# Gated outputs of batches 1 and 3 of each group: ScalarE scale and GpSimd add in the place of one VectorE instruction

## The chip, the cores and the metric

The kernel runs on one core of one Trainium2 chip. The time is the device time of that core in microseconds (us). The engines are named as in the profile: PE (TensorE; PEld is its weight load), DVE (VectorE), ACT (ScalarE), POOL (GpSimd), SP (SyncE, which issues most DMAs). [...]

## The reference

The input `x` has 16 batches of 128 tokens of 128 features, the context 16 x 77 x 128. Four layers follow each other, each with a gated cross attention and a gated feed-forward part:

```
for layer in 0..3:
    x = x + tanh(g_xattn[layer]) * attention_layer(layernorm(x), context)
    x = x + tanh(g_ffn[layer])   * ffn_layer(layernorm(x))
```

Attention has 16 heads in layers 0 to 2 and 8 in layer 3. Layer 0 multiplies its softmax by a given array `gp`. The feed-forward parts differ: in layer 0 eight experts with a threshold and a capacity, in layer 1 one expert and a second norm, in layer 2 an MLP rounded to 8 bits, in layer 3 eight experts of which each token takes one, so that tokens are sorted by expert.

## The kernel before

**Tiling.** The batches are cut into 4 groups `g` of 4 batches `i` (0 to 3). The running `x` stays in SBUF for the whole kernel: `x[g]` is a part of the tile `token[g]` (so profiles call it token), and `x[g][:, i, :]` is a tile of 128 tokens x 128 features in f32. Matrix outputs come into 4 PSUM banks of tag M, scores into 2 double banks of tag S.

**One attention group.** Layers 0 and 1 go through `small_group` (two half passes of 8 heads for each batch), layers 2 and 3 through `big_group` and `big_pass` (layer 2 has two passes of 8 heads, layer 3 has one). For each group `layer_norm` runs: statistics (DVE, L500), a few small steps (POOL, L507 to L529, and ACT, L517 and L519), the scaling to `xn` (L537 on ACT or L539 on DVE). Then `transposed` (PE tp L630, copied out at L470 on ACT or L472 on DVE). For each batch: scores S (PE, L844 or L995), their maximum and difference (DVE, L652 and L654), the exponential (ACT, L859 or L1004), sums (DVE, L864 or L1008), weighing (`gp` in layer 0 at L876, the reciprocal sums in layers 2 and 3 at L1015, on POOL or DVE), five transposes T (PE, L670) and copies to pT (ACT L470, L677 and L678, or DVE L472, L680 and L681), the product with the values. In layers 0 and 1 the reciprocal sums are spread on POOL or DVE (L887) and transposed (PE r_ps L891, copied at L895); the product O (L905) is multiplied by them on DVE (L910), and the output projection is y (L914). In layers 2 and 3 the projection is folded into the values, and y (L1021) is the product itself.

**The gate.** `gate` (L713) ends each batch and pass: one DVE instruction reads y from PSUM, multiplies it by tanh(g) and adds x, and writes x. There are 80 of these: 16 in layers 0, 1 and 3 each, 32 in layer 2. The layer norm of the next part of the layer reads all four batches of the group.

**Fillers.** Work on the context that does not depend on x, the folding of values for later layers (f_ps, L1506) and later keys (k_ps, L1678), is laid between. Layer 0's experts (h_ps L1810, y L1835) follow; some of their outputs already go the way ACT (L1848) and POOL (L1852 to L1854). At the end layer 3 sorts tokens: POOL scatters rows (L1361) to memory (rowsA for groups 0 and 1, rowsZ for 2 and 3), SP fetches blocks of rows, each goes through one expert (T L1947, h_ps L1956, y L1971), and POOL scatters the results to the output (L1980).

**What sets the order.** Every step is a node of `Work`, made by `add(at, engine, cost, fn, reads, writes, new)`, with a due time `at`, an engine or a choice of two, and a cost. `layout` is a list scheduler which runs before the program is built: it takes, of the nodes that can start, that with the earliest due time, and of two engines the one that is done first by its costs. The order that comes out is the order on each engine's queue. A node that reads a PSUM bank of tag M is due 6 units earlier. `NUDGES` shifts due times: each entry (first, count, hundredths) moves `count` nodes from `first` on; with count 0 it shifts the choice between two engines. The order on each engine is fixed when the kernel is built, and on the chip each engine takes its queue in order and waits where it must.

```
    FLEX = ("ACT", "DVE")
    ...
    add(t, WEIGH, WEIGH_COST, weigh, reads=[prk, rk], writes=[pwk], new=[("pwb", pwk)])
    ...
    add(t + 3, "DVE", 0.35, lambda i=i: gate(layer, g, i, own["y", i]), reads=[yk, ("x", g, i)], writes=[("x", g, i)])
```

Of the kernel before, what the change touches and what calls it, by code (L numbers as in the profile page):

```python
# [11 lines left out]
F32 = mybir.dt.float32  # L12
# [5 lines left out]
AF = mybir.ActivationFunctionType  # L18
ALU = mybir.AluOpType
# [3 lines left out]
P = 128  # L23
B = 16
D = 128
# [41 lines left out]
WVO = 3  # L67

# [8 lines left out]
    (1513, 6, -124), (798, 0, -181), (993, 1, -236), (1260, 1, -247), (2453, 0, -108), (1719, 2, -59), (1367, 0, -126), (993,  # L77
    6, -14), (291, 1, 107), (1571, 8, -54), (995, 1, -39), (309, 2, 221), (1529, 2, 213), (69, 4, 154), (976, 8, -55), (2180,
    4, 100), (2873, 6, -282), (995, 1, -46), (1861, 2, 51), (990, 4, -210), (741, 8, -112), (2360, 1, -288), (978, 6, -216),
    (999, 1, -97), (991, 1, -233), (1574, 1, 276), (2391, 1, 113), (987, 1, -302), (314, 8, 43), (2248, 8, -106), (861, 3,  # L80
    -155), (1142, 1, -166), (961, 1, -107), (983, 1, -234), (85, 1, 291), (1672, 4, 383), (1776, 4, -115), (2702, 8, -139),
    (1080, 3, -218), (987, 1, -109), (2728, 8, -80), (2064, 5, -279), (629, 4, 293), (336, 4, 212), (1709, 8, -65), (1048, 5,
    -247), (993, 1, 184), (742, 1, -98), (1454, 8, -130), (2724, 1, -276), (1521, 4, -278), (2207, 2, -197), (1469, 4, 62),
    (1763, 4, -247), (1520, 4, 118), (1233, 5, -233), (993, 4, 82), (1450, 6, 129), (1752, 0, -87), (2015, 0, -184), (1856,
    2, 150), (2468, 8, -390), (684, 0, -169), (2392, 6, 93), (934, 8, -326), (2721, 5, -263), (955, 1, -59), (2393, 1, -157),
    (1558, 0, -169), (1165, 0, -87), (2670, 8, -100), (2053, 0, -93), (2713, 4, -389), (961, 1, 44), (2051, 0, -126), (1993,
    4, -190), (739, 4, -167), (2308, 8, -75), (1981, 3, -237), (997, 1, -77), (948, 6, -63), (927, 8, -241), (957, 1, -52),
    (989, 3, -107), (977, 1, -150), (863, 1, 231), (2123, 1, 19), (2393, 1, 245), (2617, 4, -147), (658, 6, -53), (749, 1,
    -123), (67, 3, 289), (2690, 2, -380), (240, 4, 232), (945, 8, -73), (991, 1, 366), (997, 2, -83), (1440, 2, 180), (2021,
    1, 215), (989, 1, -132), (140, 2, 49), (2309, 4, -53), (995, 1, -35), (1676, 2, -133), (2474, 1, 237), (1001, 1, -68),  # L90
    (435, 8, 52), (2038, 4, -272), (585, 8, -283), (1675, 8, 120), (1718, 1, -396), (2152, 4, -272), (1046, 1, -307), (1754,
    2, -131), (1019, 5, -246), (852, 8, -297), (2005, 1, 104), (2393, 1, -89), (959, 1, -48), (1752, 8, 283), (2039, 5, -92),
    (974, 5, -9), (1015, 1, -67), (2393, 1, 125), (590, 0, -190), (973, 1, 13), (399, 5, -103), (2019, 1, -272), (949, 6,
    -152), (1683, 8, 40), (973, 1, -6), (1142, 1, 114), (1846, 4, 181), (1008, 4, 94), (337, 1, -32), (1005, 1, -170), (1172,
    0, -143), (955, 4, -41), (1783, 1, -182), (961, 1, -80), (2039, 6, -99), (1759, 5, -219), (581, 1, 164), (1759, 1, -268),
    (1001, 6, 24), (2484, 8, -256), (2475, 0, -193), (1757, 1, -245), (1662, 0, -75), (993, 2, 39), (2791, 6, -257), (1841,
    1, -161), (2393, 1, -66), (1581, 1, -220), (793, 0, -167), (1724, 1, -289), (1048, 1, -50), (584, 2, -262), (85, 6, -97),
    (2041, 2, 94), (2042, 4, 273), (1071, 8, -234), (578, 8, -39), (948, 5, 242), (412, 0, -161), (998, 2, 19), (1558, 8,
    -35), (2006, 0, -187), (2336, 4, -88), (2062, 1, 301), (1171, 8, 330), (1753, 4, -285), (1009, 3, -81), (2520, 4, 334),
    (1712, 5, -268), (757, 2, -48), (1014, 4, -105), (1166, 4, -383), (987, 2, 157), (1760, 8, 166), (1831, 4, 298), (1342,  # L100
    4, -369), (978, 4, 68), (989, 2, 220), (2565, 1, -363), (1001, 1, -116), (951, 3, -32), (341, 0, 185), (2065, 0, -177),
    (2269, 8, -327), (1015, 1, 34), (975, 2, -29), (747, 1, -57), (1740, 0, -107), (977, 1, -53), (966, 2, -25), (1013, 8,
    -54), (979, 1, -25), (386, 8, -205), (1003, 1, -88), (956, 2, -39), (453, 4, -276), (1514, 8, -112), (337, 1, -100),
    (953, 1, 57), (1642, 2, 385), (1003, 1, -37), (2155, 1, 187), (1046, 1, -256), (1778, 4, -39), (1982, 4, 236), (1565, 8,
    -75), (997, 2, -40), (1028, 1, 113), (993, 1, 48), (2485, 0, -178), (1460, 5, -246), (501, 2, 258), (1030, 1, -71), (742,
    1, 206), (2032, 0, -102), (977, 2, 22), (985, 1, -261), (2832, 6, -192), (337, 2, 103), (979, 4, -45), (2340, 1, -238),
    (1532, 8, -141), (742, 1, -79), (991, 1, 59), (747, 1, -134), (977, 1, 92), (998, 6, 34), (2722, 4, 319), (950, 4, -28),
    (2391, 1, 47), (948, 6, -33), (989, 1, -148), (997, 1, 101), (1684, 8, -120), (2557, 4, -242), (963, 1, -57), (336, 3,
    -107), (1028, 2, -148), (1005, 1, 209), (977, 1, -81), (959, 1, -39), (1740, 2, -302), (749, 1, -56), (749, 1, 56), (975,
    1, -77), (2186, 4, -238), (764, 1, -159), (1003, 1, -67), (977, 6, 105), (967, 1, -101), (956, 4, 31), (1013, 1, -67),  # L110
    (1046, 1, -161), (1535, 5, -90), (979, 1, -70), (1001, 1, 132), (1334, 4, -298), (1614, 3, -294), (959, 1, -45), (970, 2,
    -70), (993, 1, 58), (1005, 1, -126), (1255, 5, 161), (1008, 4, -78), (1545, 8, 310), (953, 2, 128), (984, 4, 47), (1527,
    1, -380), (958, 4, 98), (971, 2, -55), (2240, 1, -203), (997, 1, 31), (987, 1, 46), (373, 8, -112), (1003, 1, -15),
    (2216, 2, 131), (957, 1, -93), (2312, 2, -129), (714, 1, -234), (953, 4, 39), (2567, 1, -290), (1045, 5, 56), (997, 1,
    -56), (997, 2, 32), (369, 2, 100), (389, 0, -187), (1630, 1, 178), (2049, 6, -149), (744, 1, -102), (76, 8, -293), (1003,
    1, 58), (1929, 1, -214), (499, 5, -180), (456, 8, 328), (1009, 4, 74), (1005, 1, -61), (2042, 1, -226), (767, 1, -230),
    (2048, 5, -300), (2485, 8, 315), (961, 1, 29), (995, 2, -57), (2472, 6, 167), (2722, 1, -303), (2079, 8, -110), (1075, 2,
    131), (1269, 8, 150), (2045, 8, 298), (974, 4, 35), (2215, 6, -148), (1889, 2, 114), (1847, 8, 306), (1931, 1, -276),
    (682, 4, 336), (985, 1, -304), (1276, 4, 250), (970, 2, 69), (2567, 1, -242), (763, 4, -202), (989, 1, 65), (388, 5,
    -223), (995, 1, 66), (1011, 1, -250), (501, 4, -244), (1009, 3, -78), (1896, 1, 317), (1001, 4, -67), (857, 2, 172),  # L120
    (1275, 5, -157), (1013, 1, 104), (1997, 1, -179), (965, 1, -45), (1737, 4, 106), (1010, 4, -23), (2126, 2, -29), (1025,
    5, 138), (1047, 6, -61), (999, 1, -55), (2183, 2, 10), (1014, 2, 154), (1165, 4, 130), (1011, 8, -18), (2126, 3, 78),
    (638, 1, -189), (1015, 4, -128), (1010, 4, -80), (2186, 1, -234), (2580, 8, 281), (2869, 8, 365), (1587, 6, -123), (65,
    8, 60), (975, 4, 17), (1528, 5, -105), (979, 1, 179), (1009, 1, 34), (1984, 2, -283), (966, 5, 75), (995, 1, -52), (2519,
    2, 238), (2208, 1, -124), (1509, 8, -88), (2186, 1, -237), (1433, 8, -45), (2643, 4, 134), (1673, 1, -169), (1050, 4,
    137), (1019, 1, 168), (299, 2, -222), (437, 5, -50), (2415, 1, 252), (2348, 5, -96), (2277, 1, -267), (388, 4, 268),
    (2462, 2, -226), (962, 3, -300), (1005, 2, 97), (96, 0, -195), (695, 1, -300), (1446, 1, -218), (430, 1, -232), (642, 0,
    -156), (1379, 4, 379), (418, 8, 127), (2205, 2, -322), (967, 4, -103), (2336, 3, -227), (467, 5, -105), (374, 8, 127),
    (2108, 5, -69), (1003, 1, 92), (444, 3, 36), (989, 1, -81), (1046, 1, 158), (975, 1, -139), (389, 0, -199), (963, 8, 42),
    (1050, 1, -198), (2358, 1, -102), (1001, 1, -122), (965, 4, -43), (1929, 1, -152), (2128, 4, -301), (953, 4, -93), (975,  # L130
# [198 lines left out]
def kernel(ctx: ExitStack, tc: tile.TileContext, io):  # L329
# [382 lines left out]
    def gate(layer, g, i, y):  # L712
        nc.vector.scalar_tensor_tensor(x[g][:, i, :], y, tg[:, layer:layer + 1], x[g][:, i, :],  # L713
                                       op0=ALU.mult, op1=ALU.add)
# [1393 lines left out]
```

## Time and profile before

| what | value |
|---|---|
| median of 3 runs | 658.76 us (658.31 to 660.65) |
| the profiled execution's own time | 661.02 us |
| its span in the profile | 659.3 us |
| mean granted PE clock | 0.982 |
| busy: PE, DVE, ACT, POOL | 609.3, 525.2, 418.0, 326.2 us |
| DVE gates (L713) | 80, 26.4 us busy, 332 ns each |

The profile is of one execution, and its own time is above the median of the runs. A group's line gives the source line, the engine, the operation, tiles out<-in, their shapes and the count; then busy time and mean duration of one; then the time that the engine sat idle before these instructions, and what ended it. [...] "issue" is time in which an engine waited for nothing that the profile shows.

### The profile page before, as it was taken

The page shows a single profiled execution, that of the slowest core. Times are in us where ns is not written, and L with a number is a line of the kernel's source. Part 1 is how long each engine was busy: PE and PEld are TensorE (multiplying, and loading weights), DVE is VectorE, ACT ScalarE, POOL GpSimd, SP SyncE. Part 2 cuts the span into 40 slices and gives each one's busy share as a digit, 9 for nine tenths or more (in the row PEclk, how much of TensorE's full clock was granted, in tenths as well). Part 3 has the DMA queues.
Part 4 walks back from the last instruction along what each step waited for, and adds up shares of the span by engine and source line. Part 5 has one row for each costly group of instructions (what it writes and reads, how often), then busy time and mean ns, then how long its engine had stood idle before and what let it go on. Part 6 is the DMA issues. An engine that isn't in the chain of part 4 may idle for free.

```text
span 659.3 us, 16387 instructions
## 1 busy us (share of the span) xinstructions
PE 609.3 (92%) x5795; PEld 437.4 (66%) x5795; DVE 525.2 (80%) x1241; ACT 418.0 (63%) x1095; POOL 326.2 (49%) x773
## 2 busy tenths in 40 slices
PE   4888999999999999889899999999999998799895
PEld 3465666566444788555647678686667867599894
DVE  6888999994571459898998999998999999887442
ACT  3555668577666554767687857655585858347553
POOL 8687566541100106714453726528444646756653
PEclk9988999999999999998999999999999999879999
DMA  8894456748545553589574937669963532667573
GB/s 220 250 272 129 117 145 166 202 113 256 138 121 160 170 193 99 157 221 282 176 208 141 268 102 216 207 183 292 306 191 104 158 99 63 195 164 196 154 209 84
DMA packets 169179, 117.48 MB, mean 178 GB/s; under 512 B 12649, under 2 KB 159984, under 8 KB 169098
## 3 DMA queue, kind: packets, MB, share of 16 engines
q1 hardware_dynamic: 166650, 112.55, 60.1%
q0 software_dynamic: 1728, 3.17, 1.3%
q8 instruction: 46, 0.75, 0.5%
q10 hardware_dynamic: 720, 0.71, 0.4%
q14 instruction: 35, 0.29, 0.1%
HBM read 61.43 MB, written 55.89 MB: 178 GB/s over the span
## 4 chain that ended last, share of the span: by engine, by line
PE 29%; DVE 12%; POOL 7%; DMA 3%; issue 3%; ACT 2%; POOLq 0%; DVEq 0%; SPq 0%
PE y L1021 5%; PE T L670 4%; PE q_ps L951 4%; PE y L1082 2%; PE S L995 2%; POOL out_x L1980 2%; DVE pr L654 2%; DVE mx L652 2%; PE h_ps L1061 2%; PE h_ps L1956 2%; PE y L1971 1%; DVE sb L1008 1%; PE O L905 1%; DMA row<-rowsZ 1%; PE h_ps L1120 1%
## 5 line engine op out<-in xcount | busy, mean ns | idle before, releaser
L654 DVE TENSOR_TENSOR pr<-S,mx 128x616 f32<-128x616 f32 x112 | 89.6, 800 | 7.7 <-DVE mx L652 0.5
L652 DVE TENSOR_REDUCE mx<-S 128x8 f32<-128x616 f32 x112 | 87.6, 782 | 5.7 <-PE S L844 3.9
L1015 POOL TENSOR_TENSOR pw<-pr,rinv 128x616 f32<-128x616 f32 x41 | 50.0, 1225 | 71.1 <-DVE rinv L1010 33.9
L670 PE MATMUL T<-ident,pw 128*128 128x128 f32 (+1 forms) x400 | 64.0, 285 | 2.8 <-POOL pw L1015 2.5
L1021 PEld LDWEIGHTS y<-v,pT 128*128 128x128 f32 (+1 forms) x480 | 58.8, 194 | 7.4 <-issue 3.6
L1021 PE MATMUL y<-v,pT 128*128 128x128 f32 (+1 forms) x480 | 63.0, 281 | 0.2 <-DVE pT L681 0.2
L670 PEld LDWEIGHTS T<-ident,pw 128*128 128x128 f32 (+1 forms) x400 | 46.9, 143 | 23.3 <-issue 11.9
L470 ACT COPY pT<-T 128x384 f32<-128x384 f32 x99 | 46.6, 481 | 23.0 <-PE T L670 22.5
L859 ACT ACTIVATE pr<-pr 128x616 f32<-128x616 f32 x64 | 46.1, 723 | 16.0 <-DVE pr L654 15.6
L1840 DVE SCALAR_TENSOR_TENSOR token<-y,sc,token 128x128 f32<-128x128 f32 x96 | 32.9, 350 | 26.6 <-PE y L1835 23.9
L876 POOL TENSOR_TENSOR pw<-pr,gp 128x616 f32<-128x616 f32 x28 | 39.2, 1401 | 25.5 <-ACT pr L859 15.2
L864 DVE TENSOR_REDUCE ss<-pr 128x8 f32<-128x616 f32 x64 | 49.1, 783 | 1.4 <-ACT pr L859 1.4
L951 PE MATMUL q_ps<-xT,wq 128*128 128x512 f32 x96 | 48.1, 605 | 0.7 <-ACT xT L470 0.7
L677 ACT COPY pT<-T 128x128 f32<-128x128 f32 x97 | 26.7, 275 | 26.8 <-PE T L670 26.4
L470 ACT COPY vs<-f_ps 122x512 f32<-122x512 f32 (+3 forms) x56 | 32.8, 585 | 16.9 <-PE f_ps L1506 16.2
L1980 POOL DMA_INDIRECT out_x<-bo,row x30 | 29.8, 992 | 24.7 <-DVE bo L1975 19.8
L1004 ACT ACTIVATE pr<-pr 128x616 f32<-128x616 f32 x48 | 34.2, 717 | 8.0 <-DVE pr L654 7.6
L537 ACT ACTIVATE xn<-token,ln_b,ln_r 128x128 f32<-128x128 f32 x86 | 35.3, 487 | 6.2 <-POOL ln_b L529 4.0
L1506 PE MATMUL f_ps<-vz,ctxT 128*122 128x512 f32 (+3 forms) x80 | 39.1, 600 | 0.0
L1008 DVE TENSOR_REDUCE sb<-pr 128x8 f32<-128x616 f32 x48 | 37.5, 782 | 1.1 <-ACT pr L1004 1.1
L995 PE MATMUL S<-k,q 64*64 64x77 f32 x1536 | 36.0, 235 | 0.4 <-DVE pr L654 0.4
L995 PEld LDWEIGHTS S<-k,q 64*64 64x64 f32 x1536 | 31.1, 136 | 7.6 <-issue 3.2
(355 smaller groups left out, 1502.7 us busy)
## 6 DMA issues: line engine op xcount, KB each, us to landing
v<-folded SPq DMA_DIRECT2D x48, 320.0 KB
vx<-apart SPq DMA_DIRECT2D x32, 320.0 KB
apart<-vz SPq DMA_DIRECT2D x32, 308.0 KB
rowsA<-blank SPq DMA_DIRECT2D x15, 516.0 KB
rowsZ<-blank SPq DMA_DIRECT2D x15, 516.0 KB
kept<-ks SPq DMA_DIRECT2D x24, 308.0 KB
k<-kept SPq DMA_DIRECT2D x12, 616.0 KB
folded<-vs SPq DMA_DIRECT2D x21, 308.0 KB
```

Source lines behind the costliest of these rows:

```text
L470: nc.scalar.copy(out, src)
L652: nc.vector.tensor_reduce(mx, S4, axis=AX.X, op=ALU.max)
L654: nc.vector.tensor_tensor(pr.rearrange("p (a c) k -> p a c k", a=2), S4, mx.unsqueeze(3).to_broadcast([P, 2, 4, SK]), ALU.subtract)
L670: nc.tensor.transpose(own[jkey][:n, c, :], flat[:, lo:lo + n], ident)
L859: nc.scalar.activation(own["pr", i, half], own["pr", i, half], AF.Exp)
L864: nc.vector.tensor_reduce(own["s", i][:, 8 * half:8 * half + 8], own["pr", i, half], axis=AX.X, op=ALU.add)
L951: nc.tensor.matmul(own["q_ps", c], lhsT=wq()[:, (c0 + c) * P:(c0 + c + 1) * P], rhs=mem["xT"], start=True, stop=True)
L995: nc.tensor.matmul(S[rows64, a, c * SK:(c + 1) * SK], lhsT=own["q"][at, c, i * P + 64 * b:i * P + 64 * b + 64], rhs=own["k"][at, c, i * SK ...
L1008: nc.vector.tensor_reduce(s, own["pr", i], axis=AX.X, op=ALU.add)
L1015: eng.tensor_tensor(own["pw", i], own["pr", i], own["rinv", i].unsqueeze(2).to_broadcast([P, 8, SK]), ALU.mult)
L1021: nc.tensor.matmul(own["y", i], lhsT=own[u + (i, "pT", c // 3)][:n, c % 3, :], rhs=own["v", i][:n, c, :], start=(c == 0), stop=(c == 4))
L1980: ins = nc.gpsimd.indirect_dma_start(out=io["out"].rearrange("b s d -> (b s) d"), out_offset=bass.IndirectOffsetOnAxis(ap=own["row"][:, 2 ...
```

## The change

A table says which batches of a layer go the new way: batches 1 and 3 of every group in all layers. For these `gate` makes two nodes. ACT copies y out of PSUM and scales it by tanh(g) into a new SBUF tile `gt` (3 buffers), and POOL adds this tile to x. The other batches keep the DVE instruction. Both callers of `gate` now pass the due time and a function for y. The scale node reads a PSUM bank, and so is due 6 units earlier, as the DVE node is; the add on POOL does not.

`NUDGES` is another list: 733 entries for 597. Node numbers move since each changed gate is two nodes; a part of the old entries is kept under new numbers, others are dropped, many are new.

```diff
+BY_TWO = ((1, 3), (1, 3), (1, 3), (1, 3))
...
-    def gate(layer, g, i, y):
-        nc.vector.scalar_tensor_tensor(x[g][:, i, :], y, tg[:, layer:layer + 1], x[g][:, i, :],
-                                       op0=ALU.mult, op1=ALU.add)
+    def gate(at, layer, g, i, y, yk):
+
+        if i not in BY_TWO[layer]:
+            def fn():
+                nc.vector.scalar_tensor_tensor(x[g][:, i, :], y(), tg[:, layer:layer + 1], x[g][:, i, :], op0=ALU.mult, op1=ALU.add)
+            add(at, "DVE", 0.35, fn, reads=[yk, ("x", g, i)], writes=[("x", g, i)])
+            return
+        own = {}
+
+        def scaled():
+            own["t"] = lnp.tile([P, D], F32, tag="gt", name="gt", bufs=3)
+            nc.scalar.activation(own["t"], y(), AF.Copy, scale=tg[:, layer:layer + 1])
+
+        def added():
+            nc.gpsimd.tensor_tensor(x[g][:, i, :], x[g][:, i, :], own["t"], ALU.add)
+
+        tk = yk + ("t",)
+        add(at, "ACT", 0.37, scaled, reads=[yk], writes=[tk], new=[("gt", tk)])
+        add(at, "POOL", 0.5, added, reads=[tk, ("x", g, i)], writes=[("x", g, i)])
...
-            add(t + 3, "DVE", 0.35, lambda i=i: gate(layer, g, i, own["y", i]), reads=[yk, ("x", g, i)], writes=[("x", g, i)])
+            gate(t + 3, layer, g, i, lambda i=i: own["y", i], yk)
```

The last pair of lines is the same in `small_group` and in `big_pass`. `Work` is given the new tag `gt` with 3 buffers, and it is among those that are not bound to the order of due times.

## The prediction

> **What bounds the kernel now.** I read the busy times first, then the stretches, then PE's waits, and last the rows of what the change touches. The page's head:
>
> ```profile
> span 659.3 us, 16387 instructions
> ...
> PE 609.3 (92%) x5795; PEld 437.4 (66%) x5795; DVE 525.2 (80%) x1241; ACT 418.0 (63%) x1095; POOL 326.2 (49%) x773
> ```
>
> PE has 50.0 us in which it does nothing (659.3 - 609.3). The change leaves PE's work alone, so all that it can win lies in those 50.0 us. Cut at the stages, by busy time of each engine (columns: stretch, its length, PE, PEld, DVE, ACT, POOL, clock, DMA):
>
> ```profile
> 20.00:60.00 40.00, 34.27 (x299) 22.20 (x300) 34.41 (x71) 20.46 (x48) 30.35 (x49) 0.91 0.79 229
> 60.00:140.00 80.00, 77.13 (x681) 49.30 (x680) 76.06 (x155) 55.17 (x147) 47.53 (x88) 1.00 0.56 150
> 140.00:240.00 100.00, 99.94 (x418) 57.81 (x417) 53.33 (x138) 66.02 (x127) 11.55 (x23) 1.00 0.58 167
> 240.00:300.00 60.00, 52.82 (x496) 40.52 (x494) 52.93 (x133) 38.57 (x118) 30.11 (x79) 1.00 0.59 171
> 300.00:345.00 45.00, 40.95 (x369) 25.89 (x365) 40.95 (x85) 35.74 (x98) 21.57 (x59) 0.96 0.75 220
> 345.00:540.00 195.00, 192.10 (x2462) 142.64 (x2463) 179.07 (x376) 130.44 (x338) 96.94 (x279) 1.00 0.65 187
> 540.00:580.00 40.00, 32.78 (x462) 26.40 (x461) 35.80 (x106) 24.36 (x63) 26.35 (x67) 0.93 0.47 136
> ```
>
> PE is full from 140 to 240 and nearly so from 345 to 540 (2.9 us idle in 195): a DVE instruction saved there buys nothing. The first 20 us (8.6 idle) wait for loads, the last 43 (10.8 idle) for the sorted rows and the stores. What is left is 20 to 140 (5.7 + 2.9), 240 to 345 (7.2 + 4.1) and 540 to 580 (7.2): 27.1 us of PE idle, where DVE is busy 240.2 of 265 us, 91%. Who ends PE's waits (us, times, longest):
>
> ```profile
> PE S L989 <- DVE pr L654: 3.9, 1, 3.9
> PE S L840 <- DVE pr L654: 3.8, 4, 1.5
> PE r_ps L891 <- DVE r L887: 3.7, 2, 2.0
> PE r_ps L891 <- POOL r L887: 2.9, 6, 0.9
> PE tp L630 <- ACT xn L537: 2.7, 2, 2.0
> PE y L914 <- DVE aTs L910: 2.6, 4, 1.0
> ```
>
> DVE ends most of them. In these three stretches DVE is the engine to relieve.
>
> **The change, part by part.** The rows it touches (busy, mean ns of one, idle before):
>
> ```profile
> L713 DVE SCALAR_TENSOR_TENSOR token<-y,tg,token 128x128 f32<-128x128 f32 x80 | 26.4, 332 | 6.9 <-PE y L1021 3.7 <-PE y L914 2.7
> ...
> L539 DVE TENSOR_SCALAR xn<-token,ln_r,ln_b 128x128 f32<-128x128 f32 x26 | 13.1, 563 | 1.6 <-POOL ln_b L529 1.6
> ```
> ```profile
> L1848 ACT ACTIVATE yt<-y,sc 128x128 f32<-128x128 f32 x32 | 9.1, 367 | 7.6 <-PE y L1835 3.7 <-issue 1.8 <-POOL yt L1853 1.5
> ```
> ```profile
> L1015 POOL TENSOR_TENSOR pw<-pr,rinv 128x616 f32<-128x616 f32 x41 | 50.0, 1225 | 71.1 <-DVE rinv L1010 33.9 <-PE T L670 18.3 <-DVE ln_st L500 8.2
> ...
> L1854 POOL TENSOR_TENSOR token<-token,yt 128x128 f32<-128x128 f32 x8 | 3.3, 412 | 0.6
> ```
>
> *Gates.* 40 of the 80 DVE gates go: 40 x 0.332 = 13.3 us. Each becomes one ACT scale from PSUM (L1848 is that very form, 0.367) and one POOL add of 128x128 (L1854, 0.412): 14.7 us of ACT, 16.5 of POOL.
>
> *What the new order moves along.* Pieces that may run on either of two engines were placed anew. By the instruction order of both kernels DVE has 24 fewer instructions (1236 to 1212), ACT 31 more, POOL 33 more, PE and SP the same number. DVE gives 12 of its 26 layer-norm scalings (L539) to ACT and one gp product to POOL, and takes 6 weighings (L1015) and 5 spreads (L887) from POOL, and from ACT 2 wide and 6 pairs of pT copies, 4 vs, 2 wvo, 2 ks, 1 xT, 1 h. With the durations of those rows (DVE: weighing 0.904, 512 wide 0.69, pT 0.544 and 0.555 a pair; ACT: xn 0.487) DVE ends some 2 us lighter in all, not 13; ACT is about 12 us heavier (430 of 659), POOL 8 (334 of 659). Both have the room.
>
> *Where it counts.* Of the 80 gates, 14 lie in 20 to 140, 10 in 240 to 345, 7 in 540 to 580: half of 31 is 15.5 x 0.332 = 5.1 us. Of the xn scalings that leave DVE, the four at 64.1 to 66.3 (1.55 + 3 x 0.34 = 2.6) and the four at 335.4 to 337.1 (2.3) lie there too: relief 10.0. In the same stages DVE is given (orders compared between every eighth softmax maximum) 3.0 us in layer 0 (2 wvo, 1 vs, 4 spreads, 1 pT, a mask, less one gp product), 3.5 in layer 1 (4 pT pairs, xT, h, a side add, a spread, less 2 wide pT) and 2.0 in layer 3: 8.5. If all of that delays PE, the gain is 1.5; if it all falls into DVE's idle time, 10.0. DVE is 91% busy there, so I stay near the low end: 1.5 + 0.09 x 8.5 = 2.3. The spreads on DVE take 5/27 of PE's 2.9 us wait for POOL's: 0.5. Sum 2.8.
>
> *The longer way of x.* A gate now takes 0.367 + 0.412 and one hop more; the chain of waits shows 0.07 of issue between ACT's ln_r and POOL's ln_t. That is 0.85 against 0.33: 0.5 us later, and batch 3, the last of each group, is among those moved. The layer norm's statistics (L500, DVE) follow, and they now wait for POOL with the next maxima and sums queued behind them on DVE; on POOL the add stands ahead of weighings and layer-norm moments; on ACT the scale waits for PE ahead of pT copies (DVE waited 6.9 us in 80 gates, so some 3.5 go to ACT). In 140 to 240 and 345 to 540 a full PE hides this. Elsewhere it costs 0 to 0.5 for each of 12 groups (layers 0, 1, 3): 0 to 6. PE waited for a layer norm in 2 places only (the tp row above), so I take 0 for eleven groups.
>
> *The tail* is the twelfth. Both last adds stand on POOL right behind the four place2Z scatters, which ran from 586.37 to 591.21; before, DVE's last gate was done at 590.21 and the statistics at 591.81. Two adds after 591.2 end at 592.0, the last statistics at about 592.6. In the order after, a bo and a base sum that stood behind the statistics stand ahead of them, which gives back most of it: I charge 0.5 of a possible 0.8.
>
> *Due times* (597 entries become 733) add no operation. They reorder PE's rows too, which no row prices: the bounds are PE's 27.1 idle us as a gain and one more wait like L989's 3.9 as a loss. I take 0: in both orders PE has the same filler matmuls (f_ps, k_ps) ahead of the last layer-0 group and ahead of layer 1.
>
> Sum: 2.8 - 0.5 = 2.3 us. The profiled execution took 661.02 us (span 659.3 and 1.7 around it) and becomes 658.7. It stands 2.26 above the median of the runs, so the median becomes **656.5**.
>
> [...] L539 has a mean of 563 ns and yet most of its 26 take 340: a few are held up. Where, the timeline shows (start, duration):
>
> ```profile
> 64.14 2.32 DVE L539 TENSOR_SCALAR xn<-token,ln_r,ln_b 128x128 f32<-128x128 f32 x4
> 64.23 1.38 POOL L876 TENSOR_TENSOR pw<-pr,gp 128x616 f32<-128x616 f32 x1 [0.45 <-ACT pr L859]
> ```
>
> The first of the four took 1.55 us and ended with the POOL product at 65.6. The gate, which reads y from PSUM, never took over 0.352. [...] By the row, 12 of 26 such instructions leave DVE, worth 12 x (0.563 - 0.340) = 2.7, part of which is in the relief above. I keep to the sum.
>
> **Rivals.**
> - *The whole relief arrives* (0.19): what DVE is given are fillers that find idle time. Then 10.0 + 0.5 - 0.5 = 10.0 at most, 8 if a fifth is lost: median 650.8. For it: DVE ends the most PE waits. Against it: DVE is 91% busy there.
> - *The new order merely swaps loads* (0.16): DVE's total is about the same, PE's 50.0 idle us stay: 658.8.
> - *The longer way of x shows* (0.20), the case on the slower side. Place: the statistics at the group ends of layers 0, 1 and 3, held on DVE behind a POOL add. Price 0.5 each and, as DVE's queue stands still meanwhile, the relief with it. From about 6 of 12 exposed it eats the 2.8; with the add also behind a weighing of 1.2 us on POOL in three of them (3.6) and 2 bare ones (1.0): 658.8 + 4.6 = 663.4. For it: PEld's waits show tp following xn closely, so a late norm is seen. Against: POOL is idle half the time.
>
> **How the numbers follow.** The forecast (654 to 659 around 656.5) has 0.45. This kernel's measurement tells about 0.5% (3.3 us) from no change, that is 655.5 and 662.1. Of the forecast 0.18 lies under 655.5, 0.27 within. Faster: 0.18 + 0.19 = 0.37. Within: 0.27 + 0.16 + 0.02 of the slow case = 0.45. Slower: 0.18. The range reaches from the full relief to the slow case, 651.0 to 663.5; the forecast's own is 654 to 659.
>
> **What would show it.** Right: DVE's busy time falls by only 1 to 4 us; PE's idle in the three stretches falls from 27 to about 24; ACT near 430, POOL near 334. L713's successor has 40, the POOL add about 0.41 each. Wrong: PE waits at tp for xn, or DVE's L500 for the POOL add, of more than 3 us in all (the slow case); PE's idle under 20 us there (the full relief); a new gap of several us at a place that has none now (the order decides, not the gates).

## The result, and the profile after

The kernel after takes 668.45 us (median of 4 runs, 667.57 to 668.49), the kernel before beside it 659.7 (4 runs, 658.31 to 663.18). The ratio is **1.011, 95% interval 1.0076 to 1.0143: slower**, by about 1%. The forecast was 656.5, and 668.45 lies outside the range of 651.0 to 663.5. The profiled execution of after took 668.49 us, its span is 666.8, and its mean granted clock 0.976 (before: 0.982).

The head of after's page, with the line of busy times:

```profile
span 666.8 us, 16388 instructions
...
PE 606.7 (91%) x5795; PEld 436.7 (66%) x5795; DVE 526.7 (79%) x1217; ACT 427.3 (64%) x1126; POOL 336.8 (51%) x806
```

ACT and POOL took on what was expected of them. DVE did not get lighter by 2 us: it reads 1.5 more (525.2 before). PE has the same 5795 instructions and is now idle for 60.1 us (666.8 - 606.7), 10.1 more than before; its busy time is 2.6 less.

The same stretches as before (columns: stretch, its length, PE, PEld, DVE, ACT, POOL, clock, DMA):

```profile
20.00:60.00 40.00, 31.16 (x278) 19.63 (x279) 35.45 (x60) 21.05 (x58) 27.34 (x44) 0.91 0.71 203
60.00:140.00 80.00, 77.56 (x688) 49.16 (x686) 74.31 (x157) 55.25 (x146) 53.75 (x103) 1.00 0.58 160
140.00:240.00 100.00, 100.00 (x423) 58.21 (x422) 56.37 (x138) 65.01 (x129) 14.22 (x31) 1.00 0.57 164
240.00:300.00 60.00, 51.89 (x476) 40.14 (x474) 52.52 (x123) 40.30 (x122) 28.46 (x68) 1.00 0.59 175
300.00:345.00 45.00, 38.12 (x362) 25.77 (x363) 38.75 (x85) 32.53 (x90) 23.79 (x72) 0.85 0.73 217
345.00:540.00 195.00, 189.05 (x2397) 139.01 (x2395) 177.51 (x361) 136.85 (x350) 99.29 (x283) 1.00 0.64 185
540.00:580.00 40.00, 32.89 (x457) 26.19 (x454) 33.15 (x103) 23.20 (x63) 26.97 (x74) 1.00 0.39 112
```

In the three stretches where the gain was to come from (20 to 140, 240 to 345, 540 to 580) PE's idle time is 11.3 + 15.0 + 7.1 = 33.4 us; it was 27.1, and 24 was forecast. In 345 to 540, where PE had been nearly full, it went from 2.9 to 5.9. And the clock in 300 to 345 fell from 0.96 to 0.85.

Who ends PE's waits now (us in total, times, longest), of the whole span:

```profile
PE T L689 <- ACT pr L894: 6.4, 6, 2.9
...
PE S L875 <- DVE pr L673: 5.3, 5, 2.3
PE S L1024 <- DVE pr L673: 4.9, 1, 4.9
PE tp L649 <- ACT xn L556: 3.9, 2, 2.7
PE r_ps L926 <- DVE r L922: 2.3, 4, 0.7
PE tp L649 <- ACT pT L489: 2.1, 2, 1.4
...
PE tp L649 <- ACT pT L697: 1.6, 1, 1.6
```

The first row grew most. The transposes T of layers 0 and 1 wait for ACT's exponentials 6.4 us, of which 2.9 at one place (298.8 us). Before, that row read

```profile
PE T L670 <- ACT pr L859: 1.9, 5, 0.7
```

The product tp of the layer norms waits 8.7 us in all for ACT (the 3.9, 2.1 and 1.6 shown here and 1.1 for yt), against 3.0 before. What got shorter is r_ps, from 6.6 us to 4.2 (the 2.3 here, 1.1 for POOL's spreads and 0.8 for a statistic).

The trace puts the loss in time as well. I cut each trace at the starts of the 1st, 33rd, 65th, 97th and last softmax maximum (L652, L671 in after): that gives a section for layer 0 with its fillers and experts, one each for layers 1, 2 and 3, and the sorted experts at the end. Length, and PE's idle time within it (at the end: up to PE's last instruction), in us; the second and third row of after are two further profiles of it (e12, e16 below):

| | layer 0 | layer 1 | layer 2 | layer 3 | end |
|---|---|---|---|---|---|
| before | 249.1, 9.7 | 103.7, 10.3 | 136.1, 2.8 | 67.2, 7.0 | 84.0, 5.0 |
| after | 248.5, 12.8 | 109.0, 13.7 | 140.1, 5.9 | 68.2, 8.4 | 81.8, 4.2 |
| after (e12) | 249.2, 12.5 | 109.0, 13.7 | 140.3, 5.8 | 68.6, 8.5 | 88.0, 6.0 |
| after (e16) | 248.9, 12.6 | 108.7, 13.7 | 140.2, 5.8 | 69.2, 7.7 | 82.7, 3.2 |

Layer 1 is 5.3 us longer and layer 2 4.0, and three profiles agree on that within 0.3. Layer 0 is 5.3 us late at its 9th maximum, 1.3 early at the 17th, 3.1 late at the 25th and 0.6 early at the 33rd. The end varies by 6 us between profiles of one and the same kernel.

The cuts do not part the same work in both kernels. By the order on PE, ten y and two k_ps products that before does in layer 0's section stand behind the 33rd maximum in after, and ten y and three T of layer 3's section stand ahead of the 97th. So a part of what layers 1 and 2 are longer came from their neighbours: layers 0 and 1 together are 4.7 us longer, layers 2 and 3 together 5.0.

### The profile page after: what moved, and what is told of

The parts are those of the page before. It is cut to its first block, busy times and chain, and to the rows that moved or that the text cites. A ratio compares the mean times of both kernels' runs of the same rounds, so it can differ in the third digit from the quotient of the medians.

```text
span 666.8 us, 16388 instructions
## 1 busy us (share of the span) xinstructions
PE 606.7 (91%) x5795; PEld 436.7 (66%) x5795; DVE 526.7 (79%) x1217; ACT 427.3 (64%) x1126; POOL 336.8 (51%) x806
## 4 chain that ended last, share of the span: by engine, by line
PE 28%; DVE 11%; POOL 9%; issue 5%; ACT 4%; DMA 1%; POOLq 0%; DVEq 0%; ACTq 0%
PE y L1056 5%; PE T L689 5%; PE q_ps L986 4%; POOL out_x L2015 4%; PE S L1030 3%; PE y L1117 2%; PE h_ps L1096 2%; DVE pr L673 2%; DVE mx L671 2%; PE O L940 1%; ACT xn L556 1%; PE tp L649 1%; DVE sb L1043 1%; PE h_ps L1155 1%; PE S L879 1%
## 5 line engine op out<-in xcount | busy, mean ns | idle before, releaser
L671 DVE TENSOR_REDUCE mx<-S 128x8 f32<-128x616 f32 x112 | 87.6, 782 | 10.9 <-PE S L879 7.4
L1050 POOL TENSOR_TENSOR pw<-pr,rinv 128x616 f32<-128x616 f32 x35 | 42.5, 1218 | 58.0 <-DVE rinv L1045 25.5
L689 PE MATMUL T<-ident,pw 128*128 128x128 f32 (+1 forms) x400 | 62.6, 281 | 3.2 <-DVE token L735 0.9
L489 ACT COPY pT<-T 128x384 f32<-128x384 f32 x97 | 44.9, 480 | 15.5 <-PE T L689 15.1
L556 ACT ACTIVATE xn<-token,ln_b,ln_r 128x128 f32<-128x128 f32 x98 | 40.4, 485 | 11.7 <-POOL ln_b L548 10.1
L489 ACT COPY vs<-f_ps 122x512 f32<-122x512 f32 (+3 forms) x52 | 30.3, 585 | 14.0 <-PE f_ps L1541 13.5
L1870 PEld LDWEIGHTS y<-w,h 128*128 128x128 f32 x256 | 30.8, 192 | 3.9 <-issue 1.2
```

The source lines that it names most:

```text
L489: nc.scalar.copy(out, src)
L556: nc.scalar.activation(o[:, i, :], src()[:, i, :], AF.Identity, bias=mem["b"][:, i:i + 1], scale=mem["r"][:, i:i + 1])
L671: nc.vector.tensor_reduce(mx, S4, axis=AX.X, op=ALU.max)
L689: nc.tensor.transpose(own[jkey][:n, c, :], flat[:, lo:lo + n], ident)
```

## The experiments

**Theories.** A: the gates are not it; the new order of the work makes waits on PE that were not there, each at its place. B: the order is indifferent, the two-step gates cost the time (the longer way of x). Kernels tried together share a chip and its runs of the kernel before. Before took 659.7 to 665.0 us in different sittings, so only ratios are compared across them.

### Order and gates exchanged (e1, e2)

e1 keeps after's order, but each of the 40 moved gates is the old DVE instruction, issued where ACT's scale stood; nothing is issued for the add.

```diff
         def scaled():
-            own["t"] = lnp.tile([P, D], F32, tag="gt", name="gt", bufs=3)
-            nc.scalar.activation(own["t"], y(), AF.Copy, scale=tg[:, layer:layer + 1])
+            nc.vector.scalar_tensor_tensor(x[g][:, i, :], y(), tg[:, layer:layer + 1], x[g][:, i, :], op0=ALU.mult, op1=ALU.add)
         def added():
-            nc.gpsimd.tensor_tensor(x[g][:, i, :], x[g][:, i, :], own["t"], ALU.add)
+            pass
```

> The changed kernel's planned order, but the 40 moved gates are emitted as the old single DVE instruction at the place of the ACT scale, and no POOL add is issued. Theory A (the order that the new due times make is what costs): about 667, within 2 of the changed kernel's 668.5. Theory B (the two-step gate itself costs, by the longer way of x and by the load on ACT and POOL): back near the kernel before, 659 to 661.

Measured: 676.75 us beside 664.98, ratio 1.0146 (1.007 to 1.0222).

e2 keeps before's order, and the gates of batches 1 and 3 are the ACT scale and the POOL add, both issued where the DVE gate stood.

```diff
     def gate(layer, g, i, y):
+        if i in (1, 3):
+            t = lnp.tile([P, D], F32, tag="gt", name="gt", bufs=3)
+            nc.scalar.activation(t, y, AF.Copy, scale=tg[:, layer:layer + 1])
+            nc.gpsimd.tensor_tensor(x[g][:, i, :], x[g][:, i, :], t, ALU.add)
+            return
```

> The planned order of the kernel before, but the gates of batches 1 and 3 are emitted as the ACT scale and the POOL add, at the place of the DVE gate. Theory A: within 2 of the kernel before, 658 to 661, since DVE gains what the longer way loses. Theory B: 665 to 669, as slow as the changed kernel.

Measured: 668.17 beside 664.98, ratio 1.0045 (1.0009 to 1.0082).

So after's order is slow with the old gates too (layers 1 and 2 of e1: 109.9 and 139.2 us; its interval takes in after's 1.011), and A stands. But B is not nothing: in before's order the two-step gates alone cost 0.45%, some 3 us, between what A and B gave them. The longer way of x is seen in e2's waits of DVE (us, times, longest; L716 is the POOL add in this kernel):

```profile
DVE ln_st L500 <- POOL token L716: 4.3, 4, 1.7
```

Four layer-norm statistics wait 4.3 us for the add. That these waits are the 3 us is not shown: three of the four lie in layer 0, at 57, 96 and 151 us, and layer 0 of e2 takes 248.5 us, less than before's 249.1; what e2's profile has more stands in layers 1 to 3 (1.1, 2.1 and 2.0 us) and at the end. In after the same wait is there once:

```profile
DVE ln_st L519 <- POOL token L745: 0.3, 1, 0.3
```

As far as these waits go, the new order does cover the longer way of x; it loses more elsewhere.

### What the due times are worth at all (e3, e4)

Both kernels with an empty list of shifts: `NUDGES = ()`.

> The kernel before with an empty list of due-time shifts. Theory A: the lists matter much on the chip, so 670 to 690. Theory B says nothing of it but needs it as the reference for the next kernel.

> The changed kernel with an empty list of due-time shifts. Theory A: its distance to the same kernel without the two-step gate can be of either sign and is not 8. Theory B: about 8 slower than that kernel.

Measured: before 704.68 us, ratio 1.0583 (1.0493 to 1.0672); after 722.38, ratio 1.086 (1.0784 to 1.0936). The first is more than the 670 to 690 that was expected, and the distance of the two is 17.7 us, not the 8 of B. The same instructions in another order are 40 us apart in the kernel before alone (704.68 - 664.98). A term that can do this may not be entered as 0 with a loss of one wait as its worst case.

### The change made in one layer only (e5 to e8)

Here A predicts each layer from after's profile, and two rivals get letters of their own in the expectations: B, that any seam between two orders costs 3 us, and C, the longer way of x. The order is written out as a list. It follows before up to a softmax maximum, then after up to another, then before for all that is left; gates inside the part are the two-step ones (7, 8, 15 and 10 of them), gates outside the DVE instruction.

```diff
     def run(self):
-        for i in self.layout():
-            n = self.nodes[i]
-            if n["fn"] is not None:
-                n["fn"](self.on[i]) if n["many"] else n["fn"]()
+        for code in SPLICED:
+            n = self.nodes[code // 4]
+            if code % 2:
+                n["old"]()
+            elif n["fn"] is not None:
+                n["fn"](list(n["on"])[code // 2 % 2]) if n["many"] else n["fn"]()
```

> The order of before and its DVE gates, but from the start to the 32nd softmax maximum (some 268 us, layer 0's attention and the fillers beside it) the order and the two-step gates of after (7 of them). Theory A (the new order loses in some places and each loss is local): in after the softmax maxima of layer 0 were up to 5.3 us late at the 8th, but 0.6 early at the 32nd, since the full TensorE between 140 and 240 gave it back; so this gives 0 +- 1.5 us, ratio 1.000. Rival B (an order only fits itself: what follows a seam is out of step): 3 us or more, 1.005. Rival C (the longer way of x, 0.5 us for each moved gate off a full TensorE): at most 7 x 0.5 = 3.5, but hidden here by the full TensorE: 0 to 1.

> The order of before and its DVE gates, but from the 32nd to the 64th maximum (some 268 to 365 us) the order and the two-step gates of after (8 of them). Theory A: in after the maxima go from 0.6 us early at the 32nd to 4.7 late at the 64th; this alone gives +5 us, ratio 1.0075, with TensorE waits of 1.5 to 3 us near 300 and 335 and a granted clock under 0.9 behind them. Rival B: 3 us as any seam, no such waits. Rival C: 8 x 0.5 = 4 us at most, of which half is behind a busy TensorE: 2.

> The order of before and its DVE gates, but from the 64th to the 96th maximum (some 365 to 505 us) the order and the two-step gates of after (15 of them, under a full TensorE). Theory A: the maxima go from 4.7 to 8.7 us late here: +3 to +4 us, ratio 1.005. Rival B: 3 us as any seam. Rival C: 0, a full TensorE hides the longer way of x, and 15 fewer DVE gates may even gain: ratio 1.000 or 0.998.

> The order of before and its DVE gates, but from the 96th maximum to the end (some 505 us on) the order and the two-step gates of after (10 of them). Theory A: the end of after is 7.5 us late where the 96th maximum was 8.7 late: -1 us, ratio 0.998 to 1.000. Rival B: 3 us as any seam, 1.005. Rival C: 10 x 0.5 = 5 us at most, two of them in the tail: 1 to 3, ratio 1.002 to 1.005.

| part | ratio to before | its own section (length, PE idle) | that section in before |
|---|---|---|---|
| layer 0 (e5) | 1.0013 (0.9981 to 1.0045) | 249.8, 12.3 | 249.1, 9.7 |
| layer 1 (e6) | 1.0053 (1.0023 to 1.0082) | 106.8, 14.1 | 103.7, 10.3 |
| layer 2 (e7) | 1.0066 (1.0033 to 1.0099) | 138.4, 5.6 | 136.1, 2.8 |
| layer 3 (e8) | 1.0067 (1.0035 to 1.0099) | 68.6, 7.6 | 67.2, 7.0 |

Layer 0 goes as A said, and its interval ends below B's 1.005. The ratios of layers 1 and 2 do not part A (1.0075 and 1.005) from B (1.005 for any seam); the place does. e6 has after's waits at after's places (2.9 us at a T, 1.7 at another T), which B did not expect, and with before's mean clock in that section (0.984) it is 3.1 us longer there. In e7 PE waits 2.8 us more in layer 2, so a full PE does not hide its change, as C had it. Layer 3 goes against A, which expected none, and is nearer to B and C. Some 2 us of e8's loss come at its first maximum, the 97th, and so stand in layer 2's section (138.3 us, before 136.1): that is where the ten y and three T were taken ahead. A had read them as layer 2's. The four excesses add up to 1.99%, each with some 0.3% of doubt; after's own were 1.04 to 1.94% in three sittings. The profiles of e6 and e7 show one reason why such sums scatter.

**A wait that costs once one thing and once another.** Behind the part, e6 and e7 run layer 3 in the order of before, with the same waits of PE: a T that waits 1.7 us for POOL's weighing at 548 and an S that waits 3.9 us. Yet their layer 3 takes 71.3 and 71.7 us where before takes 67.2. The stretches behind these two waits (columns as above; the clock is the third from the end), first in before:

```profile
548.00:552.00 4.00, 2.27 (x15) 1.70 (x16) 3.83 (x11) 4.00 (x12) 2.60 (x4) 1.00 0.31 91
552.00:556.00 4.00, 4.00 (x27) 3.00 (x27) 3.52 (x9) 3.55 (x9) 2.51 (x9) 1.00 0.30 86
...
576.00:580.00 4.00, 3.80 (x24) 3.54 (x23) 2.89 (x9) 3.98 (x9) 0.59 (x1) 0.72 0.44 94
```

and in e7:

```profile
548.00:552.00 4.00, 2.26 (x61) 1.69 (x51) 3.83 (x10) 3.89 (x11) 2.35 (x8) 1.00 0.53 155
552.00:556.00 4.00, 4.00 (x21) 3.88 (x21) 2.72 (x7) 2.95 (x7) 2.09 (x7) 0.55 0.02 4
...
576.00:580.00 4.00, 3.15 (x63) 2.73 (x64) 3.61 (x6) 2.25 (x5) 1.42 (x3) 0.50 0.86 259
```

PE is busy for the same 2.3 us of 548 to 552 in both. Behind that, before keeps a clock of 1.00, and e7 runs at 0.55 for the next 4 us. One kernel does both: after and e16 are the same program, and in both a y waits 1.8 us for a pT copy at 559. In after:

```profile
560.00:564.00 4.00, 2.80 (x23) 2.48 (x23) 2.52 (x7) 4.00 (x10) 1.51 (x8) 1.00 0.39 110
```

in e16:

```profile
560.00:564.00 4.00, 3.12 (x15) 3.12 (x16) 1.78 (x6) 3.04 (x9) 0.63 (x3) 0.62 0.19 57
```

So a wait of 1.7 to 1.8 us was followed by a clock of 0.55 in e7 and of 0.62 in e16, and by 1.00 in before and after. The order of the work does not explain that difference; why the clock fell in one execution and not in another is not shown here. The rows suggest theory D: the new waits cost more than their own length, by the clock behind them.

### The waits filled (e9 to e12)

In front of products that wait, extra 128x128 matmuls (ident by ident) go into the bank which the product then overwrites. They fill about three quarters of the wait.

```diff
     def bank(name, shape=None):
-        return ps.tile(shape or [P, 512], F32, tag="M", name=name, bufs=4)
+        t = ps.tile(shape or [P, 512], F32, tag="M", name=name, bufs=4)
+        if work.warm:
+            count, work.warm = work.warm, 0
+            v = t[:, 0, :] if len(shape or [P, 512]) == 3 else t[:, 0:min(P, (shape or [P, 512])[1])]
+            for _ in range(count):
+                nc.tensor.matmul(v, lhsT=ident, rhs=ident[:, 0:v.shape[-1]], start=True, stop=True)
+        return t
```

> The kernel before, with 29 extra 128x128 matmuls (ident by ident, into a bank that the next real product overwrites) placed in TensorE's queue in front of six products that waited 0.9 to 3.9 us in before's profile (S at 30.8 and 567.4, r_ps at 49.4, 298.0 and 324.1, T at 548.0): they fill about three quarters of each wait and compute nothing that is used. Theory D (a wait also lowers the granted clock behind it, and that slows work that is on the path): the clock under 1 behind these places (about 10 us x (1 - clock) in before's profile) goes, the mean clock rises over 0.99, and of the 10 some half shows, since VectorE is 91% busy there too: -5 us, ratio 0.9925. Rival E (the waits alone count, the clock is made up for by other engines being late anyway): 0 to +2 us from matmuls that come at a wrong moment, ratio 1.000 to 1.003.

> The kernel after, with 54 such extra matmuls in front of nine products that waited 1.4 to 4.9 us in after's profile (tp at 19.8, 331.4 and 457.4, S at 33.7 and 576.3, T at 298.8 and 335.7, y at 558.8, n_ps at 588.1). Theory D: about 14 us x (1 - clock) stand behind these places, half of it shows: 7 us under after, so about as long as before, ratio 1.000 +- 0.003 to before. Rival E: as after, 1.011.

> The kernel after, with 12 such extra matmuls at two places alone, the T at 298.8 and at 335.7 in layer 1. Theory D: 6.8 us x (1 - clock) stood behind these two, some 3 us show: ratio 1.0065, and the maxima of layer 1 come some 3 us earlier than in after. Rival E: as after, 1.011.

> The kernel after as it is, on the same chip as the three above, as their direct measure. Both theories: ratio 1.011 to before (1.008 to 1.014).

| kernel | ratio to before, all on one chip |
|---|---|
| before, six waits filled (e9) | 0.9958 (0.9935 to 0.998) |
| after (e12) | 1.0194 (1.0159 to 1.0228) |
| after, two waits filled (e11) | 1.0129 (1.0096 to 1.0161) |
| after, nine waits filled (e10) | 1.0111 (1.007 to 1.0151) |

In after D is upheld in the main and E falls: matmuls that compute nothing make it 5.6 us faster (676.68 to 671.12; D gave 7), and 12 of them at two places in layer 1 make it 4.2 us faster (D gave 3). The ratios that were expected are missed, since after itself stood at 1.0194 here. That is 0.9% from its other two sittings, as much as the whole gain, so the times alone would be thin; the sections bear them out, as layer 1 of after takes 108.7 to 109.0 us in three profiles. What happens there is seen behind the wait at 298.8, in after:

```profile
300.00:304.00 4.00, 2.28 (x10) 1.98 (x10) 3.20 (x9) 2.13 (x7) 1.33 (x7) 0.59 1.07 313
304.00:308.00 4.00, 4.00 (x51) 2.28 (x54) 3.48 (x8) 2.55 (x10) 1.38 (x7) 0.56 1.16 281
...
336.00:340.00 4.00, 2.58 (x30) 2.10 (x30) 2.61 (x5) 3.88 (x12) 2.44 (x8) 0.50 0.63 193
```

and in e11:

```profile
300.00:304.00 4.00, 3.13 (x47) 2.15 (x47) 3.90 (x11) 2.31 (x10) 2.48 (x13) 1.00 0.99 308
304.00:308.00 4.00, 3.87 (x51) 2.81 (x52) 3.97 (x9) 3.58 (x9) 2.47 (x4) 1.00 1.01 279
...
336.00:340.00 4.00, 4.00 (x32) 2.34 (x29) 3.39 (x6) 3.55 (x8) 3.02 (x4) 1.00 0.69 224
```

The clock stays at 1.00, and layer 1 of e11 takes 105.5 us instead of 109.0 at a mean clock of 0.94. By these two profiles the lower clock costs 3.5 us in after, an estimate. But before pays there too: its layer 1 takes 103.7 us at a mean clock of 0.984, and 102.3 in e7 and e8, which run it in before's order at 1.00. At a clock of 1.00 the new order thus costs 105.5 - 102.3 = 3.2 of the 5.3 us (with the work that moved across the cut in it), and the clock the other 2.1; e6, at 0.984, says the same (3.1). So D is not all. With nine waits filled, after is still 1.5% behind before with six filled (1.0111 / 0.9958 = 1.015); its layer 2 takes 141.1 us at a clock of 1.00. And before gained 0.4%, not the 0.75% that D gave it: behind the S at 567 some 1.7 us of wait were left, and the clock still read 0.50 to 0.74 from 572 to 588. e9 is faster than both kernels in this sitting.

### Sequence and engines exchanged (e13 to e16)

103 of the 685 pieces with a choice of two engines have another engine in after. e13 is after with before's engines for them, e14 before with after's; each list is written out as above.

> The kernel after with its sequence of all pieces and its two-step gates, but each of the 103 pieces that had gone to another engine is back on the engine that before gave it (softmax weighings and sums from VectorE to GpSimd, xn from ScalarE to VectorE, pT copies both ways). Theory F (the engines that pieces were given make the waits): the sections of layers 1 and 2 fall from 109.0 and 140.1 us to about 105 and 137; ratio 1.003 to 1.006, near the 1.0045 of the two-step gates in before's order. Rival G (the sequence makes them): the sections stay at 107 to 112 and 139 to 143, ratio 1.011 or more, for the pieces now also stand on engines whose queues the sequence did not reckon with.

> The kernel before with its sequence and its 80 VectorE gates, but the same 103 pieces on the engines that after gave them. Theory F: 4 to 6 us slower, ratio 1.006 to 1.009, layers 1 and 2 about 107 and 139 us. Rival G: 0 to 2 us, ratio 1.000 to 1.003. If both this and the run before are slow, sequence and engines only fit each other, and neither is the cause by itself.

> The kernel before with 47 extra matmuls that compute nothing used: those of the first filled version, 15 for 10 in front of the S at 567.4 (there 1.7 us were left and the clock still fell to 0.5 for 14 us), 6 for 4 at 49.4, and 4, 3 and 4 in front of three products of the tail that waited for rows and weights (616, 624, 645). Theory D: another 2 to 3 us, ratio 0.991 to 0.994. Rival E: no more than the first filled version, 0.996 or above.

> The kernel after as it is, once more, as the measure of this call. All theories: 1.011 to 1.019 of before; sections of layers 1 and 2 of 109.0 and 140 us as in both profiles of it so far.

Measured: e13 1.0168 (1.0135 to 1.0202), e14 1.0253 (1.0216 to 1.0291), e15 0.9984 (0.996 to 1.0007), after (e16) 1.0104 (1.0071 to 1.0138).

F falls, and so does G. Before's engines do not mend after's sequence (layers 1 and 2 of e13: 109.2 and 139.9 us, as in after), which is what G said. But after's engines spoil before's sequence (layer 0 253.6, layer 1 108.4, layer 2 140.8) by 2.5%, where G gave 0 to 0.3% and F at most 0.9%. Both runs are slow: sequence and engines only fit each other. e13's page says one thing more:

```profile
PE 606.4 (91%) x5795; PEld 435.9 (65%) x5795; DVE 511.9 (77%) x1201; ACT 428.4 (64%) x1135; POOL 339.3 (51%) x813
```

DVE has 14.8 us less to do here than in after (526.7), of which 3.0 in layer 1 and 6.8 in layer 2, and these layers take the same time. A lighter DVE alone does not shorten them.

e15 goes as E said (0.996 or above), not as D did: its profile has a mean clock of 0.993 (before's 0.982), and its layer 3 takes 67.4 us, where before takes 67.2 at a mean clock of 0.975 in that layer. It holds e9's fillings and more, and its gain is not clear of nothing. So that e9 beats both kernels rests on one sitting, and what the clock is worth in before's layer 3 stays open.

## Why the prediction was wrong, step by step

- **The step that failed: "Due times (597 entries become 733) add no operation ... I take 0".** The bounds given were 27.1 us of gain and "one more wait like L989's 3.9 as a loss". The new order made several waits: in layers 1 and 2 the T at 298.8 (2.9 us), a tp and a T at 331 and 336 (1.5 and 1.7), a tp at 457 (1.6), and some under 1. PE's idle time in these layers rose by 3.4 + 3.1 us, and the clock behind the waits of layer 1 cost some 2 us more than in before, for which the sum had no term. The test written for it, "a new gap of several us at a place that has none now (the order decides, not the gates)", is what came; at 300.0 before had a gap of 0.7.
- **Its reason was no reason.** That the same filler matmuls stand ahead of a group does not say that PE finds something ready at every moment. The longest new wait shows it. PE's queue there, in after:

```profile
298.45 0.38 PE L834 MATMUL v_ps<-w,ctxT 128*77 128x128 f32 x2
301.72 2.40 PE L689 MATMUL T<-ident,pr 128*128 128x128 f32 x10 [2.89 <-ACT pr L894]
```

  and in before, where the T of that time stands behind other products:

```profile
298.91 0.33 PE L891 MATMUL r_ps<-ident,r 128*128 128x128 f32 x1 [0.92 <-POOL r L887]
299.17 0.87 PE L905 MATMUL O<-pT,vx 128*32 128x128 f32 x24
300.73 0.86 PE L670 MATMUL T<-ident,pr 128*128 128x128 f32 x5 [0.69 <-ACT pr L859]
```

  The tp and T at 331 and 336 show it too. ACT's queue there, in after:

```profile
328.50 1.57 ACT L894 ACTIVATE pr<-pr 128x616 f32<-128x616 f32 x2
330.83 1.65 ACT L556 ACTIVATE xn<-token,ln_b,ln_r 128x128 f32<-128x128 f32 x4 [0.76 <-POOL ln_b L548]
332.38 0.45 ACT L489 COPY pT<-T 128x384 f32<-128x384 f32 x1
...
335.74 0.69 ACT L804 ACTIVATE qs<-q_ps,qb 128x512 f32<-128x512 f32 x1 [1.08 <-PE q_ps L799]
...
336.66 0.70 ACT L894 ACTIVATE pr<-pr 128x616 f32<-128x616 f32 x1
```

  Between the exponentials from 328.5 and the next at 336.66 stand a norm's four scalings, copies, and a scaling of q for which ACT itself waits 1.08 us, since q_ps comes after the late tp. The T at 335.7 waits 1.7 us for that exponential, whose input DVE had ready at 335.0. The prediction weighed what DVE is given by counts between every eighth maximum, not by what stands between an exponential and the T that needs it.
- **The relief of 2.3 us did not arrive.** It rested on DVE ending most of PE's waits and being 91% busy. PE's idle time in the three stretches rose from 27.1 to 33.4 instead of falling to 24, and e13 has 14.8 us less on DVE than after, with layers 1 and 2 as long. Who ends a wait is the last link of a chain; the busy share does not say that a lighter engine ends it sooner.
- **The loads held for ACT and POOL, not for DVE.** ACT 427.3 (430 forecast), POOL 336.8 (334). DVE was to be 2 us lighter and reads 1.5 heavier. The durations of its instructions, added up, did fall by 2.3 us (581.9 to 579.5). But neighbours overlap, and busy time counts an overlap once: 56.7 us of it before (581.9 - 525.2), 52.8 after (579.5 - 526.7). Counts times mean durations are therefore not the change of busy time. The rows after:

```profile
L745 POOL TENSOR_TENSOR token<-token,gt 128x128 f32<-128x128 f32 x40 | 17.7, 443 | 23.8 <-ACT gt L742 22.5 <-ACT ln_lg L536 1.1
L742 ACT ACTIVATE gt<-y,tg 128x128 f32<-128x128 f32 x40 | 14.6, 366 | 21.7 <-PE y L1056 16.2 <-PE y L949 5.5
L735 DVE SCALAR_TENSOR_TENSOR token<-y,tg,token 128x128 f32<-128x128 f32 x40 | 13.3, 333 | 3.7 <-PE y L1056 3.6
L1050 DVE TENSOR_TENSOR pw<-pr,rinv 128x616 f32<-128x616 f32 x13 | 12.9, 995 | 0.4
L922 DVE COPY r<-rinvs 128x128 f32<-128x128 f32 x10 | 7.2, 719 | 0.4
L558 DVE TENSOR_SCALAR xn<-token,ln_r,ln_b 128x128 f32<-128x128 f32 x14 | 6.9, 553 | 0.7 <-POOL ln_b L548 0.7
```

  The gate's parts were sized right (366 against 367 ns, 443 against 412, 333 against 332). A weighing on DVE took 995 ns against 904, a spread 719 against 622.
- **The longer way of x, "I take 0 for eleven groups"**, held in after: one statistic waits 0.3 us for an add. In before's order the two-step gates cost 0.45% (e2), by which part of them is open. The rival "the longer way of x shows" thus named the side, and not the mechanism that decided. One of its signs did come, more than 3 us at tp for xn (3.9), but both of those waits, 1.2 us at 10.2 and 2.7 at 19.8, end before the first gate of after (42.5 us).
- **"I keep to the sum"**, which charges nothing for scalings on DVE that POOL's adds hold up, was right as far as the scalings show: the 14 that stayed on DVE take 553 ns on average, 563 before, with 40 adds more on POOL. Two of them ran beside nearly a whole add (422.4 and 465.6 us) and took 455 and 441 ns, where the four beside nothing on POOL took 335 to 348: some 0.1 us for such an add.
- **The tail's 0.5** can't be judged: the end took 81.8, 88.0 and 82.7 us in three profiles of after, 84.0 in before.

What stays open: which pieces of the sequence would have to move to mend layer 2. Its 3.1 us more of idle time come from 10 waits of 0.2 to 1.6 us where before has 4 of 0.4 to 0.75, and no run moved them singly. Which part of the two-step gates costs the 0.45% in before's order is also open.

## What to carry to other kernels

Where the order is made by due times, a changed list of them is the largest part of the change, however small the edit of the instructions is: it can be priced by walking the queues in the order after, from each product of the bounding engine back to what it needs, and the range should be wider than one wait (without the list this kernel is 40 us slower). A share of busy time says where an engine is loaded, not that relief there shortens anything. And a wait of PE in after cost more than its length, by the clock behind it (0.59 and 0.56 behind the 2.9 us at 298.8, 1.00 in e11); a few useless matmuls in front of it are a cheap test of that. They gained 0.6 to 0.8% in after; in before 0.4% in one sitting, and nothing clear in the next.

## What the hardware showed

- Behind the T that waits 2.9 us at 298.8 in after the granted clock was 0.59 and 0.56 in the two stretches from 300 to 308, and behind the T that waits 1.7 us at 548 in e7 it was 0.55 in 552 to 556; behind the S wait of 3.9 in e7 it stayed at 0.50 from 576 to 588, with PE busy for 3.15 to 4.00 us of each 4. Behind the y that waits 1.8 us at 559 it is 1.00 in 560 to 564 in one profile of after and 0.62 in another (e16).
- Some DVE and POOL instructions ran long beside each other, on both sides. In after a spread on DVE (L922) takes 1.25 us beside two products on POOL, where the median of the ten spreads is 0.387:

```profile
31.01 2.75 POOL L911 TENSOR_TENSOR pw<-pr,gp 128x616 f32<-128x616 f32 x2 [3.87 <-ACT pr L894]
31.23 1.25 DVE L922 COPY r<-rinvs 128x128 f32<-128x128 f32 x1
```

  and a 4-column step of a layer norm on POOL, 0.204 us in the median of its 38, takes 1.33 once, beside a product on DVE:

```profile
17.65 1.42 DVE L821 TENSOR_TENSOR kx<-ks,headmask 128x1232 f32<-128x1232 f32 x1
17.81 1.33 POOL L526 TENSOR_TENSOR ln_d<-ln_st 128x4 f32<-128x4 f32 x1 [4.20 <-DVE ln_st L519]
```

  That step belongs to the layer norm that PE's tp waits 2.65 us for at 19.8.
